# Graph layer 0: prologues one tile ahead, ten row chunks in place of eight, relation rows added in half chunks

## The chip, the cores and the metric

The kernel runs on one core of one Trainium2 chip, in one launch. The metric is the device time in microseconds (us), the median of three runs.

## The reference, cut to what matters

Four graph layers run over 3125 nodes with 128 features and 100000 edges; after each, the node features are added to the layer's output and normalised. The change lies in layer 0, an attention layer whose edges also carry one of 500 relation types:

```python
n = h.shape[0]
src, dst = (edge_index[0], edge_index[1])
...
z_edge = z[edge_type]
z_bar = jax.ops.segment_sum(z_edge, dst, num_segments=n)
...
pre_edge = hP1[dst] + hP2[src] + zP3[edge_type]
logit_edge = _leaky(pre_edge) @ y_w
...
ex = jnp.exp(logits - mx[dst_a])
denom = jax.ops.segment_sum(ex, dst_a, num_segments=n)
alpha = ex / denom[dst_a]
...
t_edge = hWh[src] + zWz[edge_type]
t = jnp.concatenate([t_self, t_edge], axis=0).reshape(-1, H, HD)
msg = (alpha[:, :, None] * t).reshape(-1, D)
agg = jax.ops.segment_sum(msg, dst_a, num_segments=n)
```

For each edge, one row of projected node features (picked by its source) and one row of projected relation features (picked by its type) are added. The sum gives the edge's attention logits and its message; a softmax over the edges that end in the same node weighs the messages. Layer 1 later needs, for each pair of nodes, the number of edges between them; these counts are made during layer 0, because they fit between its steps.

## The kernel before, in words

**Tiles and chunks.** The nodes are sorted by falling number of incoming edges and cut into 25 tiles of 128 nodes, one node to a partition. Tile t has CAP[t] edge slots per node, from 57 in tile 0 to 21 in tile 24. The slots are worked through in chunks of W = 8 (the last chunk of a tile is shorter), so tile 0 has 8 chunks, tile 1 has 6, tiles 2 to 11 have 5, tiles 12 to 22 have 4 and the last two have 3. A chunk is named here by tile and place: 7.3 is the fourth chunk of tile 7.

**Row gathers.** For each slot of each chunk one gather on POOL (L90, `hs<-h_tab,srcx`) brings the source's row, 264 numbers for each of 128 nodes, into the chunk's tile `hs`. There are 821 of these. `hs` tiles come from a ring of eight (`bufs=8`, L803 and L821): the row gathers of the ninth chunk wait until the first chunk's last reader is done.

**Two ways for the relation rows.** Some chunks of a tile (`by_matmul`; they hold 376 of the 821 slots) go through `multiplied`: the relation rows are picked by matmuls with one-hot matrices on PE (L838, L841, L849). The others go through `gathered` (L801 to L817): a second gather per slot on POOL (L90, `zs<-z_tab,rel`, 445 in all) brings the relation row of 328 numbers into `zs`, a ring of two tiles of 8 slots. DVE adds the first 264 numbers of all slots to `hs` in one instruction (L808), sums the last 64 over the slots by halving (L796, L799) and adds them to the tile's sum `za` (L810). In tiles 1 to 12 the chunks 0 and 2 are multiplied and the others gathered; in tiles 13 to 20, 0 and 1 are multiplied and 2 and 3 gathered; from tile 21 on chunk 0 alone is multiplied.

**Logits, softmax, spread.** Each half of a chunk is turned around on PE (L815) or built there (L841, L843), goes through DVE (L787) and ACT (L788) and a small matmul (L790) into the tile's logits. When the logits of *all* chunks of the tile are there, DVE and ACT form the softmax (L864 to L686), and `spread` (L867 to L874) multiplies each chunk's rows by their weights and sums them, one chunk after the other, starting with chunk 0. The last instruction of a chunk's spread is the addition to `ac` in L874: with it the chunk's `hs` tile is free again. So a row gather that waits for a ring place waits for the spread of a chunk eight places back, and this waits for the softmax of that chunk's whole tile.

**Prologue and closing.** `prologue(t)` (L768 to L782) zeroes and gathers the tile's own node rows `x` on POOL (L771, L90), turns them around on PE, and makes `hw` and `h1T`, which L787 needs. The closing of a tile (from L925) forms the self edge, the normalisation and the output, and ends with a scatter on POOL (L93, `x_tab<-x`).

**Counts.** Between the chunks, one step of the generator `counts` (L558 to L639) at a time, DVE makes one-hot matrices (L596, L600, `c_ohs` and `c_ohd` in L623), ACT scales some of them (L604, L605), and PE multiplies them (L608, L628).

**What sets the order.** Each engine works through a list of its own, strictly in order; an instruction whose wait isn't over holds all that stands behind it. The lists are fixed when the program is built, and the build's scheduler moves instructions against the order of the Python code. In the built list of POOL for tiles 7 and 8, for instance, the relation gathers of 7.4 are followed by those of 8.1 and 8.3 (8 each), and then by the row gathers of 8.3, 8.4, 9.0, 9.1 and 9.2, with the gather of tile 9's `x` and the scatter of tile 7 near their end, and then by the relation gathers of 8.4. Row gathers thus stand ahead of the relation gathers of the tile before.

Of the kernel before, what the change touches and what calls it, by code (L numbers as in the profile page):

```python
# [8 lines left out]
F32 = mybir.dt.float32  # L9
F16 = mybir.dt.float16  # L10
BF16 = mybir.dt.bfloat16
# [7 lines left out]
P = 128  # L19
N = 3125  # L20
NT = 25
# [6 lines left out]
W = 8  # L28
# [6 lines left out]
R = 64  # L35
HC = 2 * D + H
# [14 lines left out]
NB = [3] * 3 + [2] * (NT - 4) + [1]  # L51
CW = 512
# [23 lines left out]
def tile_gnn(ctx, tc, a, out):  # L76
    nc = tc.nc
    V, A, G, T = nc.vector, nc.scalar, nc.gpsimd, nc.tensor
# [10 lines left out]
    def gather(dst, table, idx, **kw):  # L89
        return G.indirect_dma_start(out=dst, out_offset=None, in_=table, in_offset=indirect(idx), **kw)  # L90
# [245 lines left out]
    h_tab = dram.tile([NP, HC], F32, name="h_tab")  # L336
    z_tab = dram.tile([PADREL + 1, HC + R], F32, name="z_tab")
# [147 lines left out]
    with tc.tile_pool(name="srcp", bufs=1) as sp, tc.tile_pool(name="srcq", bufs=2, space=PSUM) as ps:  # L485
# [28 lines left out]
        for o in range(0, NS, P):  # L514
            n = min(P, NS - o)
# [15 lines left out]
        blk0[nb] = late.tile([P, NT], F32, name=f"blk0_{nb}")  # L531
        G.iota(blk0[nb], pattern=[[nb * P, NT]], base=0, channel_multiplier=0, allow_small_or_imprecise_dtypes=True)
    SG = 8
    SE = max(NB) * CW // P
    each_j = slots.tile([P, NT, max(CAP)], BF16, name="each_j")
    V.tensor_copy(each_j, digits[:, :NT].unsqueeze(2).to_broadcast([P, NT, max(CAP)]))
    NAX = NT * max(NB)
# [16 lines left out]
    def counts(t, cp, ps, up):  # L554


        n, nb = CAP[t], NB[t]
# [10 lines left out]
        end = cp.tile([P, NT + 1], F32, name="c_end")  # L568
# [24 lines left out]
        for s0 in range(0, n, SG):  # L593
            k = min(SG, n - s0)
# [12 lines left out]
            for s in range(k):  # L607
                T.matmul(perm, ohb[:, :, s], oha[:, s].rearrange("p e a -> p (e a)"), start=(s0 + s == 0),  # L608
                         stop=(s0 + s == n - 1))
        ends = cp.tile([P, 2, NAX], BF16, name="c_ends")  # L610
# [3 lines left out]
        for c in range(NCW):  # L614
            w = min(CW, NP - c * CW)
            n2, e0 = nb * w // P, nb * CW // P * c
            yield
            ohs = cp.tile([P, P, SE], BF16, name="c_ohs", bufs=2)
            ohd = cp.tile([P, P, SE], BF16, name="c_ohd", bufs=2)
            for b0 in range(0, n2, SG):  # L620
                b1 = min(n2, b0 + SG)
                for to, end in ((ohs, 0), (ohd, 1)):
                    V.tensor_tensor(to[:, :, b0:b1], ends[:, end, e0 + b0:e0 + b1].unsqueeze(1)  # L623
                                    .to_broadcast([P, P, b1 - b0]), up[:, :, :b1 - b0], op=OP.is_equal)
            cps = ps.tile([P, CW], F32, name="c_ps")
            for j in range(w // P):
                for i in range(nb):
                    T.matmul(cps[:, j * P:(j + 1) * P], ohd[:, :, nb * j + i], ohs[:, :, nb * j + i],  # L628
                             start=(i == 0), stop=(i == nb - 1))
            A.activation(cs[:, c * CW:c * CW + w], cps[:, :w], AF.Copy)  # L630
        yield
        od_ps = ps.tile([P, NT], F32, name="c_od", tag="c_ps")
# [115 lines left out]
    with tc.tile_pool(name="l0", bufs=2) as wp, tc.tile_pool(name="l0s", bufs=1) as sp, \  # L748
# [19 lines left out]
        def prologue(t):  # L768

            x = wp.tile([P, D], F32, name="x")  # L770
            G.memset(x, 0.0)  # L771
            gather(x, a["x"], od.ids(t), bounds_check=N - 1, oob_is_err=False)
            xT = transposed(wp, ps1, x, "xT", "misc")
            pw = ps1.tile([P, D + HC + H], F32, name="pw", tag="misc")
            T.matmul(pw, xT, w0, start=True, stop=True)
            hw = wp.tile([P, D + HC + H], F32, name="hw")
            A.activation(hw, pw, AF.Copy)
            h1 = ps1.tile([P, P], F32, name="h1", tag="misc")
            T.matmul(h1, w0[:, :D], xT, start=True, stop=True)
            h1T = wp.tile([P, P], F32, name="h1T")  # L780
            A.activation(h1T, h1, AF.Copy)
            return x, hw, h1T  # L782
# [9 lines left out]
        def halved(v, n, last=None):  # L792

            while n > 2:
                k = n // 2
                V.tensor_add(v[:, :k], v[:, :k], v[:, n - k:n])  # L796
                n -= k
            if n == 2:
                V.tensor_add(v[:, 0] if last is None else last, v[:, 0], v[:, 1])  # L799

        def gathered(h1T, idx, rl, n, za, lg_ps):  # L801

            hs = wp.tile([P, W, HC], F32, name="hs", bufs=8)  # L803
            zs = wp.tile([P, W, HC + R], F32, name="zs")
            for s in range(n):
                gather(hs[:, s, :], h_tab, idx(s))
                gather(zs[:, s, :], z_tab, rl[:, s:s + 1])
            V.tensor_add(hs[:, :n], hs[:, :n], zs[:, :n, :HC])  # L808
            halved(zs[:, :, HC:], n)
            V.tensor_add(za, za, zs[:, 0, HC:])  # L810
            for s0 in range(0, n, 4):
                k = min(4, n - s0)
                pre = ps.tile([P, 4, P], F32, name="pre")
                for s in range(k):
                    T.transpose(pre[:, s, :], hs[:, s0 + s, :D], ident)  # L815
                logits(pre, k, h1T, lg_ps[:, s0:s0 + k])
            return hs  # L817

        def multiplied(h1T, o, n, zbT, first, lg_ps):

            hs = wp.tile([P, W, HC], F32, name="hs", bufs=8)  # L821
            for s in range(n):
                gather(hs[:, s, :], h_tab, srcx[:, o + s:o + s + 1])
            rb = wp.tile([P, W * P], F16, name="rb")
            nc.sync.dma_start(rb[:, :n * P], rel_tab[o:o + n].rearrange("(o s) p -> o (s p)", o=1)
                              .to_broadcast([P, n * P]))
            zT = wp.tile([P, W * P], F32, name="zT")
            for s0 in range(0, n, 4):
                k = min(4, n - s0)
                cols = slice(s0 * P, (s0 + k) * P)  # L830
                oh = wp.tile([P, NK, 4 * P], BF16, name="oh")[:, :, :k * P]
                zps = ps1.tile([P, 4 * P], F32, name="zps")[:, :k * P]
                for i in range(NK):
                    V.tensor_scalar(oh[:, i], rb[:, cols], relid[:, i:i + 1], None, op0=OP.is_equal)  # L834
                    parts = [(zps, zq[:, i, :2 * R]), (zps[:R], zq[:, i, 2 * R:])]
                    for z, w in parts if i < NK - 1 else parts[::-1]:
                        whole = z is zps
                        T.matmul(z, w, oh[:, i], start=(whole and i == 0), stop=(whole and i == NK - 1))  # L838
                A.activation(zT[:, cols], zps, AF.Copy)
                pre = ps.tile([P, 4, P], F32, name="pre")  # L840
                T.matmul(pre[:, :k], zw[:, :D], zT[:, cols], start=True, stop=False)  # L841
                for s in range(k):
                    T.matmul(pre[:, s, :], hs[:, s0 + s, :D], ident, start=False, stop=(s == k - 1))  # L843
                logits(pre, k, h1T, lg_ps[:, s0:s0 + k])
            for s0 in range(0, n, 3):
                k = min(3, n - s0)
                t_ps = ps1.tile([P, 3, HC - D], F32, name="t_ps")
                for s in range(k):
                    T.matmul(t_ps[:, s, :], zT[:, (s0 + s) * P:(s0 + s + 1) * P], zw[:, D:], start=True, stop=True)  # L849
                V.tensor_add(hs[:, s0:s0 + k, D:], hs[:, s0:s0 + k, D:], t_ps[:, :k])  # L850
            assert n == W
            zh = wp.tile([P, W // 2, P], F32, name="zh")
            V.tensor_add(zh, zT.rearrange("z (s p) -> z s p", p=P)[:, :W // 2],
                         zT.rearrange("z (s p) -> z s p", p=P)[:, W // 2:])
            halved(zh, W // 2, zbT if first else None)
            if not first:
                V.tensor_add(zbT, zbT, zh[:, 0])
            return hs
# [36 lines left out]
        steps = all_counts()  # L895
        n_steps = sum(4 + -(-CAP[t] // SG) + NCW for t in range(NT))
        done = 0.0
        for t in range(NT):
            n = CAP[t]
            x, hw, h1T = prologue(t)  # L900
            ac, za, _ = sums_of(t)
            lg_ps = ps1.tile([P, max(CAP), H], F32, name="lg")
            zbT = wp.tile([P, P], F32, name="zbT")
# [1 line left out]
            mults = by_matmul(t)  # L905
            for s0, w in chunks(t):
                o = OFF[t] + s0
                if s0 in mults:
                    hs = multiplied(h1T, o, w, zbT, s0 == min(mults), lg_ps[:, s0:s0 + w])
                else:  # L910
                    hs = gathered(h1T, lambda s: srcx[:, o + s:o + s + 1], rel[:, o:o + w], w, za, lg_ps[:, s0:s0 + w])
                hss.append((s0, w, hs))

                done += n_steps * w / NS
                while done > 0:
                    next(steps, None)
                    done -= 1
# [33 lines left out]
            rl = wp.tile([P, H], F32, name="rcl")  # L951
# [36 lines left out]
    with ExitStack() as ctx1, tc.tile_pool(name="l1", bufs=2) as wp, tc.tile_pool(name="l1s", bufs=1) as sp:  # L988
# [14 lines left out]
        with tc.If(general > 0):  # L1003

            with tc.tile_pool(name="l1g", bufs=1) as gp, tc.tile_pool(name="l1gp", bufs=1, space=PSUM) as ps:
# [13 lines left out]
                for t in range(NT):  # L1019
# [27 lines left out]
                    for c in range(NCW):  # L1047
                        w = min(CW, NP - c * CW)
# [5 lines left out]
                for c in range(NCW):  # L1054
                    w = min(CW, NP - c * CW)
# [6 lines left out]
        b1 = sp.tile([1, D], F32, name="b1")  # L1062
# [17 lines left out]
        for c in range(NCW):  # L1080
            w = min(CW, NP - c * CW)
# [11 lines left out]
            for i in range(w // P):  # L1093
                j = c * (CW // P) + i
# [26 lines left out]
    with tc.tile_pool(name="l2", bufs=2) as wp, tc.tile_pool(name="l2s", bufs=1) as sp, \  # L1121
# [100 lines left out]
        for t in range(NT):  # L1222
            qp = query(ps1, qb[:, t, :])
            for s0, s1, run in segments(t):
# [5 lines left out]
                n, o = s1 - s0, OFF[t] + s0  # L1230
# [7 lines left out]
            rl = wp.tile([P, H2], F32, name="rl")  # L1238
# [38 lines left out]
    with tc.tile_pool(name="l3", bufs=2) as wp, tc.tile_pool(name="l3s", bufs=1) as sp, \  # L1277
# [28 lines left out]
        for t in range(NT):  # L1306
            n = CAP[t]
# [38 lines left out]
```

## Time and profile before

| what | us |
|---|---|
| median of three runs (5845.28 to 5861.98) | 5860.65 |
| the profiled execution's own time | 4976.75 |
| its span, first to last instruction | 4975.0 |
| preparation: sorting, tables, slots | 0 to 200 |
| layer 0 with the counts | 200 to 2450 |
| layer 1 | 2450 to 2670 |
| layer 2 | 2670 to 3855 |
| layer 3 | 3855 to 4975 |

The profiled execution is 884 us shorter than the median of the runs; no view of the profile tells why. All sums are made against the profiled execution.

In a row of the table of groups, the names are out<-in, then the count, the busy time of the group and the mean duration of one in ns, and last the idle time of the engine just before them with what ended most of it. In a timeline a row has the start in us, the duration in us, the engine and the line, and in brackets the idle time of the engine before it and what ended that. Where a releaser is called "issue", nothing that the profile shows ended the wait.

### The profile page before, as it was taken

How to read it: one execution, taken by the hardware profiler on the slowest of the kernel's cores; microseconds unless marked ns; L12 is line 12 of the kernel's file. 1: busy time of each engine (PE TensorE's matmuls, PEld its weight loads, DVE VectorE, ACT ScalarE, POOL GpSimd, SP SyncE). 2: the span in 40 equal slices, each digit the busy share in tenths (PEclk: the TensorE clock that was granted, in tenths of full speed). 3: DMA queues.
4: the chain of work that ended last, by engine and by line, in shares of the span. 5: the costliest groups of instructions: out<-in, count | busy, mean ns of one | idle time of the engine just before them, and what ended most of it. 6: DMA issues, size and time to landing. Idle time of an engine off the chain costs nothing. (4 is left out here: it accounts for less than half of the span.)

```text
span 4975.0 us, 36267 instructions
## 1 busy us (share of the span) xinstructions
PE 2177.2 (44%) x10027; PEld 1321.5 (27%) x10027; DVE 3081.0 (62%) x6976; ACT 935.2 (19%) x2437; POOL 3133.7 (63%) x3136
## 2 busy tenths in 40 slices
PE   7455657675677888885490123323334000000000
PEld 5234434443444545553340011111111000000000
DVE  8545657765677778775422666666765455555556
ACT  1122323332233333331110011111112000000000
POOL 0456755666577776577005777667772777777775
PEclk9655666665676777765595555555555555555555
DMA  2433433333333443344243333333432333333332
GB/s 79 128 98 93 112 92 96 105 103 93 97 103 108 127 122 103 103 114 121 98 155 113 112 114 113 118 116 119 133 123 76 100 99 100 100 97 100 101 103 79
DMA packets 220239, 530.61 MB, mean 107 GB/s; under 512 B 65689, under 2 KB 112460, under 8 KB 215385
## 3 DMA queue, kind: packets, MB, share of 16 engines
q0 software_dynamic: 147968, 437.97, 30.6%
q1 hardware_dynamic: 72024, 89.90, 5.5%
q8 instruction: 88, 1.44, 0.1%
q14 instruction: 159, 1.30, 0.1%
HBM read 457.09 MB, written 70.63 MB: 106 GB/s over the span
## 5 line engine op out<-in xcount | busy, mean ns | idle before, releaser
L90 POOL DMA_INDIRECT hs<-h_tab,srcx x821 | 924.0, 1125 | 450.0 <-issue 334.1
L90 POOL DMA_INDIRECT kv<-kv_tab,pay_sb x821 | 783.9, 955 | 297.3 <-issue 240.4
L90 POOL DMA_INDIRECT kv<-ktv_tab,pay_sb x821 | 779.2, 949 | 282.9 <-issue 258.0
L90 POOL DMA_INDIRECT zs<-z_tab,rel x445 | 474.6, 1067 | 243.6 <-issue 122.5
L1291 DVE TENSOR_TENSOR qk<-kv,qp 128x1024 f32<-128x1024 f32 (+4 forms) x114 | 126.6, 1111 | 495.6 <-DMA kv<-ktv_tab,pay_sb 447.4
L700 DVE TENSOR_REDUCE u<-msg 128x128 f32<-128x1024 f32 (+4 forms) x228 | 383.3, 1681 | 0.0
L628 PE MATMUL c_ps<-c_ohs,c_ohd 128*128 128x128 bf16 x1300 | 334.4, 410 | 105.9 <-ACT c_sb L630 57.5
L838 PE MATMUL zps<-oh,zq 128*128 128x512 bf16 x752 | 339.6, 511 | 87.3 <-DVE oh L834 79.3
L1139 DVE TENSOR_TENSOR qk<-kv,qp 128x1024 f32<-128x1024 f32 (+4 forms) x114 | 126.5, 1109 | 369.9 <-DMA kv<-kv_tab,pay_sb 346.8
L790 PEld LDWEIGHTS lg<-yw,low 128*128 128x128 f32 x1642 | 282.0, 257 | 54.7 <-ACT low L788 37.4
L790 PE MATMUL lg<-yw,low 128*128 128x8 f32 x1642 | 278.8, 298 | 23.8 <-ACT low L788 23.3
L808 DVE TENSOR_TENSOR hs<-hs,zs 128x2112 f32<-128x2112 f32 (+7 forms) x67 | 133.1, 1987 | 234.5 <-DMA zs<-z_tab,rel 185.0
L604 ACT ACTIVATE c_oha<-c_oha,srclo 128x50 bf16<-128x50 bf16 (+2 forms) x821 | 202.5, 327 | 266.9 <-DVE c_oha L600 256.7
L696 DVE TENSOR_TENSOR msg<-kv,ex 128x1024 f32<-128x1024 f32 (+4 forms) x228 | 249.0, 1104 | 0.0
L628 PEld LDWEIGHTS <-c_ohd 128*128 128x128 bf16 x1300 | 186.4, 147 | 231.4 <-issue 88.1
L787 DVE TENSOR_TENSOR low<-pre,h1T 128x512 f32<-128x512 f32 (+1 forms) x215 | 140.2, 663 | 167.6 <-PE lg L790 60.3
L711 PE MATMUL tp<-ident,xk 128*128 128x128 f32 x100 | 43.6, 436 | 392.8 <-DVE xk L1207 388.0
L788 ACT ACTIVATE low<-low 128x512 f32<-128x512 f32 (+1 forms) x215 | 128.7, 607 | 315.2 <-DVE low L787 307.6
L1209 PE MATMUL p_ps<-wqkv,xkT 128*128 128x384 f32 x200 | 161.4, 910 | 45.5 <-ACT xkT L713 45.5
L630 ACT ACTIVATE c_sb<-c_ps 128x512 bf16<-128x512 f32 (+1 forms) x175 | 96.5, 551 | 424.8 <-PE c_ps L628 424.8
L849 PE MATMUL t_ps<-zw,zT 128*128 128x136 f32 x752 | 147.0, 327 | 60.6 <-DVE hs L850 59.6
L623 DVE TENSOR_TENSOR c_ohs<-c_ends,c_up 128x1024 bf16<-128x1024 bf16 (+4 forms) x193 | 118.8, 616 | 83.8 <-PE c_ps L628 83.6
(394 smaller groups left out, 5027.4 us busy)
## 6 DMA issues: line engine op xcount, KB each, us to landing
c_tab<-c_sb SPq DMA_DIRECT2D x25, 768.0 KB, 3.7
cs<-c_tab SPq DMA_DIRECT2D x6, 3200.0 KB, 10.9
hs<-h_tab,srcx POOLq DMA_INDIRECT x821, 2.8
kv<-kv_tab,pay_sb POOLq DMA_INDIRECT x821, 2.7
kv<-ktv_tab,pay_sb POOLq DMA_INDIRECT x821, 2.7
rb<-rel_tab SPq DMA_DIRECT2D x47, 256.0 KB, 3.6
zs<-z_tab,rel POOLq DMA_INDIRECT x445, 2.9
h_tab<-h SPq DMA_DIRECT2D x25, 132.0 KB, 1.9
```

Of the source, the lines that this page charges most:

```text
L90: return G.indirect_dma_start(out=dst, out_offset=None, in_=table, in_offset=indirect(idx), **kw)
L604: A.activation(oha[:, s, 0, :], oha[:, s, 1, :], AF.Copy, scale=srclo[:, o:o + 1])
L628: T.matmul(cps[:, j * P:(j + 1) * P], ohd[:, :, nb * j + i], ohs[:, :, nb * j + i], start=(i == 0), stop=(i == nb - 1))
L696: V.tensor_tensor(msg[:, :n, :].rearrange("p s (h d) -> p s h d", h=heads), val.rearrange("p s (h d) -> p s h d", h=heads), ex.unsqueeze(3 ...
L700: V.tensor_reduce(u, msg[:, :n, :].rearrange("p s d -> p d s"), AX.X, OP.add)
L787: V.tensor_add(low[:, :k], pre[:, :k], h1T.unsqueeze(1).to_broadcast([P, k, P]))
L788: A.activation(low[:, :k], low[:, :k], AF.Relu)
L790: T.matmul(lg_ps[:, s, :], low[:, s, :], yw8, start=True, stop=True)
L808: V.tensor_add(hs[:, :n], hs[:, :n], zs[:, :n, :HC])
L838: T.matmul(z, w, oh[:, i], start=(whole and i == 0), stop=(whole and i == NK - 1))
L849: T.matmul(t_ps[:, s, :], zT[:, (s0 + s) * P:(s0 + s + 1) * P], zw[:, D:], start=True, stop=True)
L1209: T.matmul(p_ps, xkT, wqkv[:, k, :], start=(k == 0), stop=(k == NTY - 1))
```

## The change

The change lies in the stage of layer 0 and in the counts that run beside it, in five places.

- The ring of `hs` has ten tiles in place of eight.
- In `gathered`, `zs` has room for 4 slots in place of 8, still in a ring of two. A chunk is worked in two halves: row and relation gathers of up to 4 slots, then the addition to these `hs` slots, the halving and the addition to `za`.
- `prologue(t + 1)` is called ahead of the last chunk of tile t; `prologue(0)` is called ahead of the loop.
- In `counts`, the one-hot tiles `c_ohs` and `c_ohd` have 8 columns in place of 12 (SE = 8). Where NB[t] is 3 (the first three tiles), 12 columns are made as 6 and 6 in two pairs of tiles in place of 8 and 4 in one pair. Where it is 2 or 1, the pieces stay as they were.
- The PSUM tile `cps` is asked for ahead of these and not after them.

```diff
-    SE = max(NB) * CW // P
+    SE = 8
...
-            ohs = cp.tile([P, P, SE], BF16, name="c_ohs", bufs=2)
-            ohd = cp.tile([P, P, SE], BF16, name="c_ohd", bufs=2)
-            for b0 in range(0, n2, SG):
-                b1 = min(n2, b0 + SG)
+            cps = ps.tile([P, CW], F32, name="c_ps")
+            for b0 in range(0, n2, SE // nb * nb):
+                b1 = min(n2, b0 + SE // nb * nb)
+                ohs = cp.tile([P, P, SE], BF16, name="c_ohs", bufs=2)
+                ohd = cp.tile([P, P, SE], BF16, name="c_ohd", bufs=2)
...
         def gathered(h1T, idx, rl, n, za, lg_ps):
-            hs = wp.tile([P, W, HC], F32, name="hs", bufs=8)
-            zs = wp.tile([P, W, HC + R], F32, name="zs")
-            for s in range(n):
-                gather(hs[:, s, :], h_tab, idx(s))
-                gather(zs[:, s, :], z_tab, rl[:, s:s + 1])
-            V.tensor_add(hs[:, :n], hs[:, :n], zs[:, :n, :HC])
-            halved(zs[:, :, HC:], n)
-            V.tensor_add(za, za, zs[:, 0, HC:])
+            hs = wp.tile([P, W, HC], F32, name="hs", bufs=10)
+            for s0 in range(0, n, W // 2):
+                k = min(W // 2, n - s0)
+                zs = wp.tile([P, W // 2, HC + R], F32, name="zs")
+                for s in range(k):
+                    gather(hs[:, s0 + s, :], h_tab, idx(s0 + s))
+                    gather(zs[:, s, :], z_tab, rl[:, s0 + s:s0 + s + 1])
+                V.tensor_add(hs[:, s0:s0 + k], hs[:, s0:s0 + k], zs[:, :k, :HC])
+                halved(zs[:, :, HC:], k)
+                V.tensor_add(za, za, zs[:, 0, HC:])
...
         def multiplied(h1T, o, n, zbT, first, lg_ps):
-            hs = wp.tile([P, W, HC], F32, name="hs", bufs=8)
+            hs = wp.tile([P, W, HC], F32, name="hs", bufs=10)
...
+        ahead = prologue(0)
         for t in range(NT):
             n = CAP[t]
-            x, hw, h1T = prologue(t)
+            x, hw, h1T = ahead
...
             for s0, w in chunks(t):
                 o = OFF[t] + s0
+                if s0 + w == n and t + 1 < NT:
+                    ahead = prologue(t + 1)
```

More of the change, by code (lines that the diff above doesn't have):

```diff
@@ L617, in counts @@
             yield
-            ohs = cp.tile([P, P, SE], BF16, name="c_ohs", bufs=2)
-            ohd = cp.tile([P, P, SE], BF16, name="c_ohd", bufs=2)
-            for b0 in range(0, n2, SG):
-                b1 = min(n2, b0 + SG)
+            cps = ps.tile([P, CW], F32, name="c_ps")
[3 more added lines that the diff above has]
+                ohd = cp.tile([P, P, SE], BF16, name="c_ohd", bufs=2)
                 for to, end in ((ohs, 0), (ohd, 1)):
-                    V.tensor_tensor(to[:, :, b0:b1], ends[:, end, e0 + b0:e0 + b1].unsqueeze(1)
+                    V.tensor_tensor(to[:, :, :b1 - b0], ends[:, end, e0 + b0:e0 + b1].unsqueeze(1)
                                     .to_broadcast([P, P, b1 - b0]), up[:, :, :b1 - b0], op=OP.is_equal)
[L625 to L629, printed above, removed]
+                for b in range(b1 - b0):
+                    j, i = divmod(b0 + b, nb)
+                    T.matmul(cps[:, j * P:(j + 1) * P], ohd[:, :, b], ohs[:, :, b], start=(i == 0), stop=(i == nb - 1))
             A.activation(cs[:, c * CW:c * CW + w], cps[:, :w], AF.Copy)
```

## The prediction

> **What bounds the kernel now.** I read the busy time by windows first, then the table of groups, then timelines of POOL and DVE around the end of one tile. h(7.3) and z(7.3) below mean the row gathers and the relation gathers of chunk 3 of tile 7. By windows (busy us of each engine, then the granted clock), no engine fills layer 0:
>
> ```profile
> 490.00:1425.00 935.00, 620.46 (x3161) 404.34 (x3161) 628.59 (x1544) 286.39 (x770) 603.23 (x545) 0.64 0.36 99
> 1425.00:2290.00 865.00, 693.72 (x3433) 445.27 (x3432) 661.29 (x1761) 295.04 (x763) 611.24 (x564) 0.70 0.41 115
> ```
>
> PE, DVE and POOL are each busy 65 to 80% of both windows: they wait for each other. The groups say where POOL and DVE stand still:
>
> ```profile
> L90 POOL DMA_INDIRECT hs<-h_tab,srcx x821 | 924.0, 1125 | 450.0 <-issue 334.1
> L90 POOL DMA_INDIRECT zs<-z_tab,rel x445 | 474.6, 1067 | 243.6 <-issue 122.5
> L808 DVE TENSOR_TENSOR hs<-hs,zs 128x2112 f32<-128x2112 f32 (+7 forms) x67 | 133.1, 1987 | 234.5 <-DMA zs<-z_tab,rel 185.0
> ```
>
> POOL is idle 693.6 us ahead of 1266 gathers. About 0.30 us ahead of each is regular (380 us); the other 314 us are waits. DVE waits 185 us for relation rows. The timelines show both as one loop. DVE at the end of tile 7:
>
> ```profile
> 1130.58 0.98 DVE L808 TENSOR_TENSOR hs<-hs,zs 128x792 f32<-128x792 f32 x1 [15.77 <-DMA zs<-z_tab,rel]
> ...
> 1164.96 1.22 DVE L872 TENSOR_TENSOR hs<-hs,lgs 128x1024 f32<-128x1024 f32 x1
> ...
> 1169.59 0.29 DVE L874 TENSOR_TENSOR az<-az,hs 128x128 f32<-128x128 f32 x1
> ```
>
> And POOL:
>
> ```profile
> 1170.62 5.90 POOL L90 DMA_INDIRECT hs<-h_tab,srcx  x1 [21.96 <-PE pre L843]
> ...
> 1212.87 0.95 POOL L90 DMA_INDIRECT hs<-h_tab,srcx  x1 [0.30 <-issue]
> 1214.12 0.95 POOL L90 DMA_INDIRECT hs<-h_tab,srcx  x1 [0.30 <-issue]
> ...
> 1230.57 1.02 POOL L93 DMA_INDIRECT x_tab<-x,node_d  x1 [0.30 <-issue]
> 1231.89 0.96 POOL L90 DMA_INDIRECT zs<-z_tab,rel  x1 [0.30 <-issue]
> 1233.15 0.95 POOL L90 DMA_INDIRECT zs<-z_tab,rel  x1 [0.30 <-issue]
> ```
>
> DVE stood 15.77 us for z(7.4), the last rows of tile 7. From their issue (end 1128.6) to the last spread instruction of 7.0 (1169.9) it is 41 us; call this L. POOL did z(8.1) and z(8.3) meanwhile, then stood 21.96 us at h(8.3), the ninth chunk after 7.0: the name PE L843 was long done, the ring place came with L874, 0.7 us before. Then POOL does 40 DMAs up to z(8.4), and DVE waits again. So a tile takes L plus the DMAs from the waiting gather to the last relation gather of the next tile. For tiles 1 to 11, L is 32 to 47 us.
>
> **What the skill says.** "Perfetto Trace Analysis", GPSIMD Engine Instruction, says to time POOL by start to start and not by reported spans. The trace bears it out: a gather lasts 0.95 us, but follows in 1.25 (1212.87, 1214.12). "SBUF — State Buffer", Who interferes with whom, says that a DVE tensor_tensor with two SBUF inputs contends with reads of GpSimd, and infers that it doesn't hinder descriptor generation. These gathers read their indices from SBUF, and the one beside the spread lasts 5.90 us; the measurement decides, so I price gathers inside the loop: 1170.62 to 1234.1 is 63.5 us for 40, or 1.59; tiles 2 to 10 treated so give 1.39 to 1.6, mean 1.5. Tiles 13 to 15, with no long wait, take 48 DMAs in 66 us, or 1.38. "Perfetto Trace Analysis", Optimizing Scalar/DVE Operations, gives about 60 ns of cost per DVE instruction, and some 120 as latency; the 2112 and 1056 wide additions take 2361 and 1256 ns by form, so splitting one costs about 150 ns: more than the first, near the second.
>
> **The change part by part.**
>
> *Half chunks.* A full gathered chunk takes one 2361 ns addition, halvings of 414, 286 and 218, and one 216 for `za`: 3.50 us. After: two of 1256, 286, 218 and 216: 3.95. For 45 full chunks that is 20 us of DVE; most lies where DVE waits for z anyway, and I take 5 on the path (0 to 20).
>
> *Ring of two half chunks, ring of ten.* Here the built lists decide, not the text. z of a half waits for the half two before it, so the scheduler holds z back and lets h run ahead, as ten places allow. POOL's list from the last z of a tile to the h that waits for that tile's chunk 0, and on to the last z of the next tile:
> - tile 7 before: z(7.4), 16 z of 8.1 and 8.3, then h(8.3) waits for 7.0; 40 DMAs follow. After: z(7.4), only 8 z of 8.1, then h(9.0) waits for the same 7.0; 47 follow.
> - tile 14 before: z(14.3), 46 DMAs (h of 15, x, a scatter, z of 15), then h(16.0) waits for 14.0, nearly done. After: z(14.3), 8 z of 15.2, then h(16.2) waits for 14.0; 38 follow, h(16.2) to h(17.1), x, a scatter and z(15.3).
>
> So h stalls two chunks later in count, but behind its blocking gather now stand z(8.3) or z(15.3), which DVE needs. The cover of L falls from 16 (once 18) to 8 gathers in tiles 1 to 9, and from 40 or more in tiles 12 to 20. After, it is 8 in every tile from 1 to 21 but one (12 there).
>
> New L: the DVE instructions in its list from the addition of a tile's last z to the spread of chunk 0, priced with the rows of before, come to 26 us on average over tiles 1 to 21 (22 to 34; count and one-hot work included). The same sum for tiles 2 to 11 of before is 10.5 us below the measured L (waits for PE, ACT and the landing). So L is about 36.6 us, 21 times: 769. DMAs after the wait: 457 in tiles 1 to 9 (389 before), 460 in tiles 10 to 21; 917 at 1.45 (between 1.38 and 1.5): 1330. Together 2099 us from the last z of tile 1 to that of tile 22, against 2286.9 - 489.7 = 1797 now: +302. By stretch: tiles 1 to 9 some +90, tiles 10 to 21 some +210, as each tile there goes from 66-70 us to about 90. Bounds: L from 30 to 42 gives -140 to +115; the price 1.38 to 1.5, -64 to +46. Tile 0 and the tail I take as even: 16 more h stand ahead of tile 0's last z (+20), the tail has some 20 gathers fewer (-20), and DVE sets its length.
>
> *Prologue.* On POOL a memset (0.22) and a gather (1.02), on PE six passes (0.3 to 0.8 us each), on ACT three copies (0.27, 0.50, 0.27): none added or removed, and none on SP, whose loads of the tile's sums stay where they were. Its PSUM tiles share one ring place with the closing's. On POOL, the x gather is now behind two more chunks of h, still ahead of the scatter of tile t-2, and ahead of the previous tile's last z in place of the tile's own. Its ring of two makes it wait for the closing two tiles back, for which the scatter beside it waits anyway. It can end DVE's waits for h1T (32.7 us, 15 times, at most 4.3), most of them beside PE work; I take -10 (-33 to +5: two more DMAs ahead of the last z, a wait for that PSUM place).
>
> *Counts.* 8+4 columns cost 682+811+411+543 ns for both ends, 6+6 by interpolation the same. Waits for the ring average 1.3 us, at most one more in 21 blocks: 0 to +27, I take +3.
>
> Sum: 302 + 5 - 10 + 3 = +300. Own time 4976.75 to about 5277. The median of the runs is 884 us longer, and the profile doesn't tell where. If all were stretched alike, +300 would be +353; if PE alone were slower, later tiles would already be held by it and the loss some 200. I add 300 unchanged: 5860.65 + 300 = 6160. A few tenths of a per cent are what a measurement of this kernel can tell from no change; I use 0.3%.
>
> **Rivals.**
>
> *Backlog covers the wait* (0.17). In tiles 13 to 20 DVE and PE are busy about 80%. If they carry unfinished work through POOL's wait, later tiles stay at 66-70 us and only tiles 1 to 9 lose: +100, 5960. For it: DVE runs late there now, 60 to 80 us from last z to spread. Against: in the new list the next tile's z(3) is behind the stalled h, so that backlog drains.
>
> *The loop gets shorter: faster* (0.09). The wait after is L less the cover of 8 gathers at 1.45, 11.6 us. Over 22 tiles this equals the 314 us of today at L = 26 us. Should half chunks and the early h1T cut L under that, the ring of ten wins; at 16 us, a chain with no foreign work in it (in the DVE timeline: addition to logits, 1130.58 to 1136.5, 6; the softmax's own rows and its wait for ACT 5; spread, 1164.96 to 1169.88, 5), the waits are some 100 and the time 5650. For it: the sum of DVE work is just 26. Against: L was never under 31 in tiles 1 to 11, where it is equally awaited.
>
> *Nothing moves* (0.06): what h(t.3) waited is waited at the new place, DVE and PE keep their 76 to 80%; 5860.
>
> **How the numbers follow.** Main case 0.68, 6160, mostly 6040 to 6330 (L and price above, and the factor to the runs). Backlog 0.17, 5890 to 6040. The range 5900 to 6330 leaves out the faster and the even case and the ends of the others, about 2 in 10. Slower by over 0.3%: 0.85; within: 0.06; faster: 0.09.
>
> **What would show it.** Right: POOL waits of 20 to 30 us once per tile from tile 1 to 21, ahead of h, ending within 2 us of an L874-like addition, 8 z after a tile's last z; later tiles at 85 to 95 us; DVE's wait for z well above 185 us; layer 0 longer by some 300 us, other stages even. Wrong: L under 26, or tiles 13 to 20 still near 68 us. The split additions are right if they take near 1.26 us, 90 of them from full chunks.

## The result and the profile after

| | median, us | runs | lowest to highest |
|---|---|---|---|
| before | 5862.26 | 10 | 5845.28 to 5869.19 |
| after | 5887.23 | 10 | 5878.19 to 5910.56 |

The ratio is 1.0053 (95% interval 1.0037 to 1.0069). The change makes the kernel slower, as forecast, but by 25 us and not by 300.

The experiments below bear on every number here, so one finding comes first: the kernel before, unchanged, takes 4969 to 4979 us in some measurements and 5843 to 5909 in others. Within one measurement its runs agree. I call these the first and the second condition. The profile that the prediction was worked out from is of the first; the times before and after, and the profile after, are of the second.

Table of groups, kernel after (busy and mean ns, then the idle time ahead and what ended most of it):

```profile
L90 POOL DMA_INDIRECT hs<-h_tab,srcx x821 | 891.4, 1086 | 651.7 <-issue 483.3
L90 POOL DMA_INDIRECT zs<-z_tab,rel x445 | 447.4, 1005 | 758.7 <-DVE az L811 250.6
L809 DVE TENSOR_TENSOR hs<-hs,zs 128x1056 f32<-128x1056 f32 (+2 forms) x121 | 140.7, 1163 | 68.2 <-DMA zs<-z_tab,rel 64.9
```

POOL's idle time ahead of gathers has doubled against the profile before: 1410 us, 694 there. A little over half of it is ahead of relation gathers; the largest share there, 250.6 us, is ended by `az` of L811, the instruction that frees a half buffer `zs`. DVE's wait for relation rows did not grow, it shrank, from 185 to 64.9 us. Busy time by windows, kernel after, from the last relation gather of tile 1 to that of 10, and on to that of 22:

```profile
560.00:1761.00 1201.00, 650.60 (x3136) 426.93 (x3137) 628.21 (x1594) 285.01 (x769) 568.69 (x539) 0.60 0.28 76
1761.00:2997.00 1236.00, 732.84 (x3444) 476.74 (x3444) 662.07 (x1815) 292.60 (x765) 593.89 (x573) 0.62 0.29 80
```

DVE does as much as before (1290 us in both together), but PE, DVE and POOL are busy only 47 to 59% of the time. Timeline of POOL, kernel after, around the end of tile 7:

```profile
1361.12 1.15 POOL L90 DMA_INDIRECT zs<-z_tab,rel  x1 [15.70 <-DVE az L811]
...
1369.01 0.95 POOL L90 DMA_INDIRECT zs<-z_tab,rel  x1 [0.30 <-issue]
1373.97 0.94 POOL L90 DMA_INDIRECT zs<-z_tab,rel  x1 [4.01 <-DVE az L811]
...
1377.71 0.95 POOL L90 DMA_INDIRECT zs<-z_tab,rel  x1 [0.31 <-issue]
1412.52 5.90 POOL L90 DMA_INDIRECT hs<-h_tab,srcx  x1 [33.85 <-PE pre L844]
```

And of DVE:

```profile
1371.94 0.97 DVE L809 TENSOR_TENSOR hs<-hs,zs 128x792 f32<-128x792 f32 x1
...
1411.49 0.28 DVE L875 TENSOR_TENSOR az<-az,hs 128x128 f32<-128x128 f32 x1
```

This is the forecast picture: z(7.4), only 8 relation gathers of 8.1 behind it, then h(9.0) stands 33.85 us and goes 0.7 us after the spread of 7.0. New are the 15.70 us ahead of z(7.4), which no step of the prediction has.

### The profile page after: what moved, and what is told of

Its sections match the earlier page's. It is cut to its first block, busy times and chain, and to the rows that moved or that the text cites. A ratio compares the mean times of both kernels' runs of the same rounds, so it can differ in the third digit from the quotient of the medians.

```text
span 5886.5 us, 36435 instructions
## 1 busy us (share of the span) xinstructions
PE 2246.3 (38%) x10027; PEld 1369.1 (23%) x10027; DVE 3117.5 (53%) x7129; ACT 933.7 (16%) x2437; POOL 3067.2 (52%) x3136
## 5 line engine op out<-in xcount | busy, mean ns | idle before, releaser
L90 POOL DMA_INDIRECT hs<-h_tab,srcx x821 | 891.4, 1086 | 651.7 <-issue 483.3
L90 POOL DMA_INDIRECT zs<-z_tab,rel x445 | 447.4, 1005 | 758.7 <-DVE az L811 250.6
L789 PE MATMUL lg<-yw,low 128*128 128x8 f32 x1642 | 303.5, 313 | 124.3 <-ACT low L787 80.2
L789 PEld LDWEIGHTS lg<-yw,low 128*128 128x128 f32 x1642 | 304.6, 274 | 170.4 <-ACT low L787 104.1
L624 DVE TENSOR_TENSOR c_ohs<-c_ends,c_up 128x1024 bf16<-128x1024 bf16 (+5 forms) x193 | 118.9, 616 | 363.0 <-remote 217.9
L842 PE MATMUL pre<-zT,zw 128*128 128x512 f32 x188 | 145.3, 864 | 122.0 <-ACT zT L840 87.8
L809 DVE TENSOR_TENSOR hs<-hs,zs 128x1056 f32<-128x1056 f32 (+2 forms) x121 | 140.7, 1163 | 68.2 <-DMA zs<-z_tab,rel 64.9
```

The source lines that it names most:

```text
L789: T.matmul(lg_ps[:, s, :], low[:, s, :], yw8, start=True, stop=True)
```

## The experiments

Ratios are to the kernel before in the same measurement, with 95% intervals. The waits are the sums, in layer 0, of POOL's idle times of over 0.8 us ahead of relation gathers (z) and row gathers (h), in one profile each; the end is the start of layer 0's last scatter, that of tile 24.

| kernel | condition | time, before beside it | ratio | z, h waits | end |
|---|---|---|---|---|---|
| before, first profile | 1 | 4977 (profiled) | | 113, 208 | 2447 |
| before | 1 | 4970, 4973 | 0.999 (0.998 to 1.000) | 112, 211 | 2442 |
| before | 2 | 5843, 5854 | | 603, 341 | 3059 |
| after, first profile | 2 | 5887, 5862 | 1.0053 | 638, 411 | 3108 |
| after | 1 | 5270, 4972 | 1.059 (1.057 to 1.062) | 325, 396 | 2742 |
| prologue ahead alone | 1 | 5147, 4973 | 1.035 (1.032 to 1.037) | 301, 248 | 2618 |
| prologue ahead alone | 2 | 5856, 5909 | 0.991 (0.989 to 0.993) | 556, 387 | 3070 |
| halves, two half buffers, eight places | 1 | 5235, 4973 | 1.052 (1.050 to 1.054) | 219, 430 | 2700 |
| the same | 2 | 5944, 5854 | 1.015 (1.013 to 1.017) | 689, 437 | 3159 |
| halves, two half buffers, ten places | 2 | 5937, 5845 | 1.015 (1.012 to 1.017) | 712, 413 | 3152 |
| after with eight places | 1 | 5275, 4973 | 1.061 (1.058 to 1.063) | 324, 398 | 2739 |
| halves, four half buffers, eight places | 2 | 5864, 5854 | 1.002 (1.001 to 1.003) | 563, 445 | 3072 |
| the same | 1 | 4965, 4979 | 0.997 (0.996 to 0.998) | 30, 309 | 2438 |
| halves, five half buffers, eight places | 1 | 4883, 4979 | 0.981 (0.979 to 0.982) | 9, 236 | 2363 |

**The kernel before and the kernel after, again** (no edit).

> The kernel before, unchanged, for a second profile. Theory A (the timed runs of before already stood in long waits, which its one profiled execution of 4975 us did not have): a span near 5860, layer 0 near 2880 and not 2250 us, layers 2 and 3 together near 2550 as in the profile after, and POOL's waits of over 0.8 us ahead of row and relation gathers in layer 0 well above the 321 us of the first profile, some 700 to 1000. Theory B (the first profile shows layer 0 as it runs, and the other 884 us lie elsewhere): layer 0 near 2250, POOL's waits near 320, and layers 2 and 3 or what surrounds the span longer by 884.

Measured: 4969.77, before 4972.97; a copy of the first profile. By itself it seemed to speak for theory B; but the kernel before, too, took 4973 in this measurement and not 5862. So neither theory was tested, and the 884 us turned out to depend on the measurement.

> The changed kernel, unchanged, once more beside the kernel before. In the first four experiments the kernel before took 4973 us and not 5862, so the 890 us belong to the conditions of the first measurement and not to the kernel. Theory A (those conditions slowed every release and so hid the change's own waits; where before takes 4973 the change costs what its parts cost): 5200 to 5330, the prediction's own sum being 5277. Rival (the change is worth the same half per cent everywhere, and eight places or the separate parts are what is bad in the other kernels): 4980 to 5020.

Measured: 5894.64 beside 5844.68, ratio 1.0082 (1.0060 to 1.0103). The second condition had come back, so this told nothing of the first.

> The kernel before, unchanged, for a profile. Two conditions have shown: before at 4973 us, and at 5845. Where it takes 5845, Theory A says that layer 0 is near 2860 us (5845 less the 200, 222, 1340 and 1215 us of the other stages as the profile after has them), that POOL's waits of over 0.8 us ahead of row and relation gathers in layer 0 are some 700 to 950 and not 321, so that the waits which the change was to bring are there already, and that DVE's semaphore updates come at least 0.7 us apart in the bursts at the end of a tile. Rival: layer 0 near 2250 with waits near 321, the rest in layers 2 and 3. Where it takes 4973, it only repeats the first profile.

Measured: 5842.75. Theory A held: layer 0 ends near 3060, and its waits are 944 us. Groups of this run of the kernel before:

```profile
L90 POOL DMA_INDIRECT hs<-h_tab,srcx x821 | 889.3, 1083 | 582.6 <-issue 400.7
L90 POOL DMA_INDIRECT zs<-z_tab,rel x445 | 457.8, 1029 | 729.4 <-DVE az L810 444.9
```

The idle time is 1312 us, 694 in the first condition: the same code waits as long as the kernel after. Its POOL at the end of tile 7 (the relation gathers of 8.1 follow z(7.4); in the first profile none of them waited):

```profile
1349.02 0.95 POOL L90 DMA_INDIRECT zs<-z_tab,rel  x1 [0.31 <-issue]
1358.06 0.95 POOL L90 DMA_INDIRECT zs<-z_tab,rel  x1 [8.09 <-DVE az L810]
...
1404.98 5.91 POOL L90 DMA_INDIRECT hs<-h_tab,srcx  x1 [26.69 <-PE pre L843]
```

Beside these gaps stand late releases. They are plainest for DVE in layer 2, a stretch that the change doesn't touch, first in the first profile of before, then in this one:

```profile
3602.73 0.28 DVE L1207 TENSOR_SCALAR xk<-xqb,is_t 128x128 f32<-128x128 f32 x1
3602.92 0.28 DVE L701 TENSOR_TENSOR accb<-accb,u 128x128 f32<-128x128 f32 x1
3603.12 1.21 DVE L696 TENSOR_TENSOR msg<-kv,ex 128x1024 f32<-128x1024 f32 x1
3604.26 0.28 DVE L1207 TENSOR_SCALAR xk<-xqb,is_t 128x128 f32<-128x128 f32 x1
3604.45 1.88 DVE L700 TENSOR_REDUCE u<-msg 128x128 f32<-128x1024 f32 x1
```

```profile
4329.74 0.43 DVE L1207 TENSOR_SCALAR xk<-xqb,is_t 128x128 f32<-128x128 f32 x1
4332.71 0.29 DVE L701 TENSOR_TENSOR accb<-accb,u 128x128 f32<-128x128 f32 x1 [2.54 <-remote]
4332.91 1.22 DVE L696 TENSOR_TENSOR msg<-kv,ex 128x1024 f32<-128x1024 f32 x1
4334.05 0.28 DVE L1207 TENSOR_SCALAR xk<-xqb,is_t 128x128 f32<-128x128 f32 x1
4336.92 1.88 DVE L700 TENSOR_REDUCE u<-msg 128x128 f32<-128x1024 f32 x1 [2.59 <-issue]
```

The durations are equal. But an instruction that needs a result of DVE itself starts 2.8 to 3.0 us after that result's recorded end (L701, L700), where it started 0.1 us after it. The updates of DVE's semaphore in this stretch are recorded at 4324.98, 4325.69, 4327.08, 4327.78, 4331.28, 4332.68, 4334.09: always a multiple of 0.70 us apart, to within 0.02, where the other profile has gaps down to 0.08. "Perfetto Trace Analysis" of the Trainium skill, DVE / Act Engine Instruction, puts the recorded end at the moment the engine pushes its update and the spreading of the update after it; so this delay lies outside every busy time, and a table of busy times can't show it. Such stretches, of six updates or more, stand in layers 2 and 3 (26 of them) and not in layer 0.

In layer 0, where the change lies, it is PE's updates that come late. The same run, two groups of passes of PE and the instructions of DVE and ACT that need them:

```profile
1985.28 0.96 PE L849 MATMUL t_ps<-zw,zT 128*128 128x136 f32 x6 [1.51 <-issue]
1986.08 2.02 PE L628 MATMUL c_ps<-c_ohs,c_ohd 128*128 128x128 bf16 x8
2005.72 0.58 DVE L850 TENSOR_TENSOR hs<-hs,t_ps 128x408 f32<-128x408 f32 x1 [18.71 <-remote]
2014.85 0.60 ACT L630 ACTIVATE c_sb<-c_ps 128x512 bf16<-128x512 f32 x1 [28.20 <-remote]
```

("remote" is an update that no end recorded in the 1.5 us before it explains.) The passes were over by 1988.1; the updates of PE's semaphore that let DVE and ACT go on are recorded at 2005.70 and 2014.82. In layer 0, 56 waits of DVE, 434 us together, ended so on an update of PE, and none in the first profile. All engines have fewer separate updates on record here: DVE 4684 (6145 in the first profile), PE 2006 (2296), ACT 1178 (1641). That these delays make POOL's new gaps is argued from the order of the lists; no run took them away alone. From the start of layer 2 to the end this run takes 252 us more than the first profile (2557 against 2305), up to there 614 more (3284 against 2670).

> The changed kernel, unchanged. Where before takes 4973, Theory A: 5200 to 5330 (the prediction's sum: 5277), with POOL's waits ahead of row and relation gathers in layer 0 near 620 us. Rival (the change is worth half a per cent in either condition): 4980 to 5020. Where before takes 5845: 5885 to 5900 again.

Measured: 5886.12 beside 5854.34, ratio 1.0064 (1.0043 to 1.0086): the second condition again.

> The changed kernel, unchanged. Where before takes 4973, Theory A: 5200 to 5330 (the prediction's sum is 5277), with POOL's waits ahead of row and relation gathers in layer 0 near 620 us. Rival (the change is worth half a per cent in either condition): 4980 to 5020. Where before takes 5845: 5885 to 5900 again, which tells nothing new.

Measured: 5269.75 beside 4972.25, **+5.9%**: the first condition at last. Theory A held, within 8 us of the prediction's own sum, though term by term it fits less well (told further down); the waits are 721 and not 620. Groups:

```profile
L90 POOL DMA_INDIRECT hs<-h_tab,srcx x821 | 904.9, 1102 | 636.8 <-issue 514.3
L90 POOL DMA_INDIRECT zs<-z_tab,rel x445 | 451.2, 1014 | 449.7 <-DVE az L811 124.8
L809 DVE TENSOR_TENSOR hs<-hs,zs 128x1056 f32<-128x1056 f32 (+2 forms) x121 | 140.8, 1164 | 253.5 <-DMA zs<-z_tab,rel 236.4
```

The idle time of POOL went from 694 to 1087 us, and DVE's wait for relation rows from 185 to 236.

**The prologue alone**, put into the kernel before:

```diff
+        ahead = prologue(0)
         for t in range(NT):
-            x, hw, h1T = prologue(t)
+            x, hw, h1T = ahead
...
+                if s0 + w == n and t + 1 < NT:
+                    ahead = prologue(t + 1)
```

> The kernel before with the prologue issued one tile ahead, nothing else. The prediction's price is -10 (-33 to +5): 5828 to 5867. A rival (the early x gather and the copies stand ahead of work that the loop waits for): +20 or more.

Measured: 5146.91 beside 4972.97, +174 us. The rival held. POOL's list is nearly that of before; what is new is a wait of PE. The longest waits of PE in this run (total us, times, longest):

```profile
PE tp L711 <- DVE xk L1210: 395.7, 33, 25.8
PE tp L711 <- DMA x<-in_x,node_d: 327.1, 24, 26.9
```

and in the kernel before, second measurement:

```profile
PE tp L711 <- DVE xk L1207: 384.6, 32, 25.7
PE tp L711 <- DVE an L1185: 198.9, 19, 32.1
```

PE's first pass of the next tile's prologue now waits 24 times for the gather of `x`. That gather is queued on POOL behind the row gathers that wait for a ring place, and on PE everything of the present tile that stands behind the pass waits too. In the kernel before, no wait of PE for this gather is on record.

> The kernel before with the prologue one tile ahead, nothing else. Where before takes 4973: 5147 again. Where before takes 5845, Theory A (the waits which it brings are there already): 5790 to 5870, since between the kernels with half chunks and ten places the early prologue gained 43 us there; the rival (it costs the same in both conditions): near 6020.

Measured: 5149.92 beside 4972.25, ratio 1.0345 again.

> The kernel before with the prologue one tile ahead, nothing else. Where before takes 5845, Theory A (the waits which it brings are there already): 5790 to 5870; the rival (it costs the same in both conditions): near 6020. Where before takes 4972: 5150 again.

Measured, second condition: 5855.98 beside 5909.28, **faster** by 0.9%. Theory A said that the loss would be absent here, and it is; why there is a gain was not found. It is one measurement, in which the kernel before took 55 to 66 us more than in the others of this condition. PE's recorded waits for `x` are 89 us there.

**Half chunks of relation rows and count blocks of eight alone** (the change without the early prologue, and with `bufs=8`).

> Half chunks of relation rows and count blocks of eight alone; eight places, the prologue at the start of its own tile. Theory A: 5880 to 5930, as after or slightly more. Rival C: 5990 or more. Rival D: under 5860.

Measured: 5234.67 beside 4972.97, +262. The three numbers had been written around 5862 and can't be used. Rival D (ten places do the harm) falls in any case, since eight lose as well.

> Half chunks with two half buffers, eight places, the prologue in its own tile. Where before takes 4973: 5235 again. Where before takes 5845, Theory A (late releases leave POOL waiting in any case): between 5860 and 5940, so at most a third of the 262 us; the rival (each part costs the same in both conditions): near 6105.

Measured, second condition: 5944.17 beside 5854.34, +90: theory A's line (5940, or 87) missed by 3 to 4 us, the rival's by 160.

**Ten places or eight.** The change with eight, and the change without the early prologue with ten:

```diff
-            hs = wp.tile([P, W, HC], F32, name="hs", bufs=10)
+            hs = wp.tile([P, W, HC], F32, name="hs", bufs=8)
```

> After with eight places in the ring of row chunks in place of ten; half chunks and early prologues stay. Theory A (the loop is held by the ring of relation halves and by late releases, as much as by the ring of rows): the ring hardly matters, 5880 to 5930. Rival C (ring of ten is the part that gains, half chunks the part that loses): 100 us or more above after, 5990 or more. Rival D (ten places let the rows run too far ahead of the relation rows, as the prediction said): faster than after, 5800 or less.

Measured, first condition (its numbers too were written around 5862): 5274.90 beside 4972.97, ratio 1.061; with ten it is 1.059.

> Half chunks and ten places, the prologue at the start of its own tile. With eight places this took 5235 beside 4973 of before. Theory A (the ring of relation halves decides how far POOL gets, the ring of rows does not): 5180 to 5250. Rival C (ten places give POOL back the distance): 5100 or less. Rival D (ten places put more rows ahead of the awaited relation rows): 5280 or more.

Measured, second condition, while its numbers are for the first: 5937.21 beside 5844.68, ratio 1.015; with eight it is 1.015. So beside two half buffers the ring of ten does nothing that can be measured, for good or ill. The likely reason, that the ring of two `zs` stops POOL first, was not tested: ten places beside four or five half buffers were not tried.

**Four and five half buffers** (as many and more relation rows than before), eight places, the prologue in its own tile unless said (for five, `bufs=5`):

```diff
-                zs = wp.tile([P, W // 2, HC + R], F32, name="zs")
+                zs = wp.tile([P, W // 2, HC + R], F32, name="zs", bufs=4)
```

> Half chunks with four half buffers of relation rows in place of two (as many rows held as before), eight places, the prologue one tile ahead. With two half buffers this took 5275. If the loss of the half chunks is the halved store of relation rows: near 5147, the prologue alone (5110 to 5180). If it is the halving itself (more and smaller additions): still 5250 to 5290.

This one has the early prologue. Measured, second condition, while the numbers are for the first: 5861.76 beside 5844.68, ratio 1.0028 (1.0017 to 1.0039), the same as without the early prologue, which follows.

> Half chunks with four half buffers, eight places, the prologue at the start of its own tile. If the loss of the half chunks is the halved store: near the 4973 of before (4930 to 5010), a little less if half chunks release rows earlier. If it is the halving itself: 5200 or more.

Measured, second condition: 5861.11, ratio 1.0026 (1.0015 to 1.0036).

> Half chunks with four half buffers of relation rows, eight places, the prologue in its own tile. Where before takes 4973: if the loss of the half chunks (262 us with two half buffers) is the halved store, 4930 to 5010; if it is the halving itself, 5200 or more. Where before takes 5845: 5861 again.

Measured, second condition: ratio 1.0020 (1.0007 to 1.0032).

> Half chunks with four half buffers of relation rows, eight places, the prologue in its own tile. Where before takes 4972: if the loss of the half chunks is the halved store, 4930 to 5010; if it is the halving itself, 5200 or more. Where before takes 5845: 5861 again.

Measured, second condition, with before at 5909: ratio 0.998 (0.997 to 0.999).

> Half chunks with four half buffers of relation rows, eight places, the prologue in its own tile. Where before takes 4972: if the loss of the half chunks is the halved store, 4930 to 5010; if it is the halving itself, 5200 or more. Where before takes 5845 to 5910: 0.2% slower to 0.2% faster, as twice measured.

Measured, first condition: 4964.52 beside 4978.59, ratio 0.997. The 262 us are gone: it was the halved store, not the halving. Its POOL is held much less ahead of relation gathers (30 us of long waits, 219 with two half buffers):

```profile
L90 POOL DMA_INDIRECT zs<-z_tab,rel x445 | 451.3, 1014 | 163.4 <-issue 116.7
```

With two half buffers the same row was:

```profile
L90 POOL DMA_INDIRECT zs<-z_tab,rel x445 | 453.8, 1020 | 345.5 <-issue 115.3
```

> Half chunks with five half buffers of relation rows (ten columns of 128 rows in place of the eight of before), eight places, the prologue in its own tile. If the store of relation rows is what holds POOL's gathers back: faster than four half buffers, where before takes 4972 by 10 to 60 us, where it takes 5845 by 20 to 100. If it is the ring of row chunks or the wait for their release alone: within 10 us of four half buffers.

Measured, first condition: 4883.35 beside 4978.59, **-1.9%** (1.8 to 2.1), 81 us less than with four half buffers in the same measurement, more than either theory had. Its rings take 93824 bytes of a partition (8 x 8448 + 5 x 5248), those of the kernel after 94976. Its groups:

```profile
L90 POOL DMA_INDIRECT hs<-h_tab,srcx x821 | 926.2, 1128 | 478.6 <-issue 357.5
L90 POOL DMA_INDIRECT zs<-z_tab,rel x445 | 469.6, 1055 | 143.4 <-issue 116.7
```

This version beats both kernels in the first condition; in the second it was not measured.

## Why the prediction was wrong

*The step that failed is "I add 300 unchanged".* The sum was made on a profiled execution of 4977 us, and the loss carried over to runs of 5861 as if the missing 884 us lay beside it. Most of them lie in layer 0 itself, which ends 612 us later (3059 against 2447), the others in layers 2 and 3. In the second condition the kernel before already waits 603 us at z and 341 at h in layer 0, where the sum had 113 and 208. The early wait which half chunks bring takes the place of waits that are there: z and h waits grow by 105 us there (638 + 411 against 603 + 341), in the first condition by 400 (325 + 396 against 113 + 208). A tile of 17 to 20 takes 67 us before and 82 after in the first condition, 94 and 96 in the second. That waits take each other's place is read from these sums. The whole change, at 297 us in the first condition and 32 to 50 in the second in experiments, and half chunks alone, at 262 and 90, go the same way. The prediction gave 353 and 200 as the other ways to carry its number over; neither is near 25. The prediction says itself that the profile doesn't tell where the 884 us lie: that was the place to widen the range down to no change.

*Rings and half chunks, +302: near where the profile was taken, and the close total is partly luck.* There, POOL stands ahead of a row gather in each of the tiles 1 to 21, 8 relation gathers after a tile's last one, and goes 0.7 us after the spread that frees the place: the loop of the prediction. The stretch from tile 1's last relation gather to tile 22's is 2134 us (2099 in the sum) against 1791 in the kernel before, measured again. L averages 33.2 us over tiles 1 to 21 (36.6 in the sum); the 917 DMAs cost 1.57 us each (1.45), with 155 us of long waits ahead of relation gathers among them, which the sum counted as nothing. Tile 0 gives 9 us more, and the part after tile 22 takes 108 us against 160. So the end of layer 0 moves by 343 + 9 - 52 = 300 us. But this is the whole change. Half chunks without the early prologue cost 262 us where the sum has 302 + 5; the early prologue beside them costs 40 where it has -10. Two misses of some 45 and 50 us cancel.

*Its cause was put too wide.* The term named two rings. The halved store of relation rows is the cause: four half buffers take the loss away in the first condition, eight places in the other ring change nothing.

*Halved additions, 5 on the path.* 1.25 us each, 102 of them of that size; with four half buffers the same additions cost nothing that shows in the total.

*Prologue, -10 (-33 to +5): wrong in both conditions.* Alone it costs 174 us in the first and gains some 53 in the second. Beside two half buffers it costs 40 in the first (5275 against 5235) and gains 43 in the second (5895 against 5937); beside four, in the second, it does nothing (1.0028 against 1.0026). The step followed the x gather on POOL, and what it would delay there. It did not ask who waits for its landing, and what stands behind that one on PE.

*Counts, +3.* Not measured alone; with four half buffers they and the halves together lose nothing in the first condition.

*The rivals.* "Nothing moves" is nearest in number. Its reason, that what h(t.3) waited is waited at the new place while the engines keep their share, is half right: h waits grow only from 341 to 411, but the larger part had already been waited at z, and the engines are busy about half of the time, not 76 to 80%. "Backlog covers the wait" and "faster" gave no time near the result. Of the signs named ahead, the waits once per tile came true in both conditions (10 to 35 us). The others came true in the first alone: tiles 13 to 20 at 88 us (70 before), DVE's wait for z at 236, layer 0 longer by 300. In the second, such tiles take 105 us, but 98 in the kernel before too; DVE's wait for z is 65, and in place of it DVE waits 440 us in layer 0 for updates of PE that come late; layer 0 is longer by 49.

*What stays open:* what the second condition is, and why updates are late in it. It came and went between measurements, at the same code, and isn't a matter of one chip: the chip that the record numbers 5 showed the first condition, then the second, then the first again. The granted clock was lower too (0.58 against 0.61), but rows of DVE with equal durations and 2.5 us of idle time between them speak against that clock as the cause. Whether the missing updates were merged or only not recorded is not known. Why the early prologue gains there is open as well.

## What to carry to other kernels

If the profiled execution and the timed runs differ by far more than the runs among themselves, take no difference from that profile before the gap has a place: waits that a change brings are worth only what is not waited there already. Count a ring by the rows that it holds and not by its places: here, pieces of half the size needed twice the buffers to lose nothing. A step that is moved early must be followed to who waits for its data, and to what stands behind that one.

## What the runs showed of the hardware

The same program took 4970 us in some measurements and 5840 to 5910 in others. In the second, DVE's instructions have equal durations in the stretch shown, but updates of semaphores come late: in layers 2 and 3 DVE's, at multiples of 0.70 us there, so that an instruction on DVE's own result starts up to 3 us after it; in layer 0 PE's, by 19 and 27 us in the lines shown. I had not expected release times to depend on anything but the program.
